# Decay-weighted graph aggregation on one core: decay weights from a scan per row, against decay weights from counts made by matmuls

## The chip, the core and the metric

The kernel runs on one core of a Trainium2 chip. Engines: PE (TensorE, matrix products), DVE (VectorE), ACT (ScalarE), POOL (GpSimd) and SP, which here only issues loads. The time is the device time of one execution in microseconds; the kernel before took 437.13 us (median of three runs, 437.13 to 437.59).

## The reference

```python
h = jnp.maximum(_layernorm(x, axis=-1), 0.0)        # x is (4096, 64)
support = h @ weight                                # weight is (64, 64)
mask = (adj != 0).astype(support.dtype)             # adj is (4096, 4096), fp32
rank = jnp.cumsum(mask, axis=1)
deg = rank[:, -1:]
k = jnp.minimum(deg, float(MAX_NEIGH))              # MAX_NEIGH = 100
pos = rank - (deg - k)
w = mask * jnp.where(pos > 0, DECAY ** (k - pos), 0.0)   # DECAY = 0.5
return x + (w @ support + bias)
```

A neighbour of row i with c neighbours behind it in the same row gets the weight 2^-c, and 0 from the hundredth on. `adj` is 67 MB and is the only large input.

## The kernel before

Rows of `adj` go through in 32 tiles of 128 rows. A tile is one load of 2 MB (`a_sb`, L165, three buffers, issued by SP). Two DVE instructions make the weights of a tile. The mask (L167) writes `f`, 1/2 at a neighbour and 1 elsewhere, in bf16. The scan (L169) runs along each row from its end, `S[j] = max(f[j] * S[j+1], floor)`, in bf16, in one of two buffers. The weight is a difference, S[j+1] - S[j].

PE needs the weights with the column of `adj` on the partitions. For each of 32 column blocks of a tile it multiplies two shifted pieces of S by the identity and by minus the identity and adds them in PSUM (L177, L178): transpose and difference at once. ACT copies eight blocks at a time to SBUF as bf16 (`wT`, L179). PE then multiplies each block with the support of its 128 columns (L148, 192 columns, since the fp32 support is three bf16 parts). The result `po` of a tile is copied by ACT (L153), and POOL adds the three parts and x plus bias (L157, L158, L159) and stores four tiles at a time (L161).

Ahead of this stand the loads of x, weight and bias on ACT's queue (L61 to L66), the layernorm on DVE (L88 to L107), its transpose on PE (L118), the product with the weight (L131) and the split into three parts (L134 to L137). Each engine takes its instructions in the order in which the framework put them; on DVE the layernorm stands among the first masks and scans.

Of the kernel before, what the change touches and what calls it, by code (L numbers as in the profile page):

```python
# [19 lines left out]
def kernel(  # L20
# [50 lines left out]
    ident_b = const.tile([P, P], BF16, name="ident_b")
    nc.gpsimd.tensor_copy(ident_b, ident)
    nident_b = const.tile([P, P], BF16, name="nident_b")
    nc.gpsimd.tensor_scalar_mul(nident_b, ident, -1.0)
    floor_sb = const.tile([P, 1], F32, name="floor_sb")
    nc.gpsimd.memset(floor_sb, 2.0 ** -(MAX_NEIGH - 1))
    S_bufs = []
    for b in range(2):
        S = const.tile([P, N + 1], BF16, name=f"S{b}")
        nc.gpsimd.memset(S[:, N:N + 1], 2.0)  # L80
        S_bufs.append(S)

# [1 line left out]
    def rows(t):  # L84
        return t.unsqueeze(2).to_broadcast([P, C, D])

    mean = setup.tile([P, C], F32, name="mean")
    nc.vector.reduce_sum(mean, x_sb, axis=AX.X)  # L88
    nc.vector.tensor_scalar_mul(mean, mean, 1.0 / D)
    xc = setup.tile([P, C, D], F32, name="xc")  # L90
    nc.vector.tensor_sub(xc, x_sb, rows(mean))  # L91
    sq = setup.tile([P, C, D], F32, name="sq")
    nc.scalar.activation(sq, xc, AF.Square)  # L93
    var = setup.tile([P, C], F32, name="var")
    nc.vector.reduce_sum(var, sq, axis=AX.X)
    nc.vector.tensor_scalar(var, var, 1.0 / D, EPS, op0=ALU.mult, op1=ALU.add)
    # 1 / sqrt(var), with a Newton step for the last bits: y * (1.5 - 0.5 * var * y * y)
    rstd = setup.tile([P, C], F32, name="rstd")
    nc.scalar.activation(rstd, var, AF.Sqrt)
    nc.vector.reciprocal(rstd, rstd)  # L100
    corr = setup.tile([P, C], F32, name="corr")
    nc.vector.tensor_mul(corr, var, rstd)
    nc.vector.tensor_mul(corr, corr, rstd)
    nc.vector.tensor_scalar(corr, corr, -0.5, 1.5, op0=ALU.mult, op1=ALU.add)
    nc.vector.tensor_mul(rstd, rstd, corr)
    hn = setup.tile([P, C, D], F32, name="hn")
    nc.vector.tensor_mul(hn, xc, rows(rstd))  # L107

    xb = const.tile([P, C, D], F32, name="xb")
    nc.gpsimd.tensor_add(xb, x_sb, bias_sb.unsqueeze(1).to_broadcast([P, C, D]))  # L110

# [1 line left out]
    hT = setup.tile([P, C // 2, P], F32, name="hT")  # L113
    for g in range(C // 2 // G):
        pt = ps_t.tile([P, G, P], F32, tag="pt", name=f"pth{g}")
        for k in range(G):
            a = g * G + k
            nc.tensor.transpose(pt[:, k, :], hn[:, 2 * a:2 * a + 2, :].rearrange("p c d -> p (c d)"), ident)  # L118
        nc.scalar.activation(hT[:, g * G:(g + 1) * G, :], pt, AF.Relu)  # L119

    sup = const.tile([P, C, 3, D], BF16, name="sup")
    CS = G * P // D
    for g in range(C // CS):
        pt = ps_t.tile([P, G, P], F32, tag="pt", name=f"pts{g}")
        # the two row halves of hT go to one bank each
        pv = pt.rearrange("p (s h) (q d) -> p s (h q) d", s=2, d=D)
        part = sup[:, g * CS:(g + 1) * CS].rearrange("p (k s) e d -> p s k e d", s=2)
        for k in range(CS // 2):
            a = g * (CS // 2) + k
            for s in range(2):  # L130
                nc.tensor.matmul(pv[:, s, k, :], hT[s * D:(s + 1) * D, a, :], w_sb[s * D:(s + 1) * D, :],  # L131
                                 start=True, stop=True)
        rest = setup.tile([P, 2, CS // 2, D], F32, name="rest", bufs=2)
        nc.scalar.activation(part[:, :, :, 0, :], pv, AF.Copy)  # L134
        nc.vector.tensor_sub(rest, pv, part[:, :, :, 0, :])  # L135
        nc.scalar.activation(part[:, :, :, 1, :], rest, AF.Copy)
        nc.vector.tensor_sub(part[:, :, :, 2, :], rest, part[:, :, :, 1, :])  # L137

# [1 line left out]
    out_t = out.rearrange("(c p) d -> p c d", p=P)  # L140
    osb = None
    pending = None

    def aggregate(po, wT, t, g):
        nonlocal osb
        for k in range(G):
            c = g * G + k
            nc.tensor.matmul(po, wT[:, c, :], sup[:, c].rearrange("p s d -> p (s d)"),  # L148
                             start=(c == 0), stop=(c == C - 1))
        if g < NG - 1:  # L150
            return
        parts = work.tile([P, 3, D], F32, name="parts")
        nc.scalar.activation(parts, po.rearrange("p (s d) -> p s d", d=D), AF.Copy)  # L153
        if t % OG == 0:
            osb = work.tile([P, OG, D], F32, name="osb")
        o = osb[:, t % OG, :]
        nc.gpsimd.tensor_add(parts[:, 1, :], parts[:, 1, :], parts[:, 2, :])  # L157
        nc.gpsimd.tensor_add(parts[:, 0, :], parts[:, 0, :], parts[:, 1, :])  # L158
        nc.gpsimd.tensor_add(o, parts[:, 0, :], xb[:, t, :])  # L159
        if t % OG == OG - 1:  # L160
            nc.gpsimd.dma_start(out_t[:, t - OG + 1:t + 1, :], osb)  # L161
# [50 lines left out]
```

## Time and profile before

| | |
|---|---|
| median of three runs | 437.13 us |
| span of the profiled execution | 435.5 us |
| time around the span (median less span) | 1.6 us |
| DVE busy | 370.5 us, 85% of the span |
| POOL busy | 331.3 us, 76% |
| PE busy | 255.4 us, 59% |
| ACT busy | 148.8 us, 34% |
| mean granted TensorE clock | 0.863 of full speed |
| loads of adj | 67.11 MB, 42.1% of the time of the 16 DMA engines |

Busy time counts an engine as busy from the start of an instruction to its end, whether it computes or is held. Matmuls overlap, so PE's mean duration of one is longer than the distance between two starts; rates are read from starts. In the timeline, "x8" is a run of eight like instructions, the second number is the length of the run, and "[... <-...]" is the idle time ahead and what ended it.

### The profile page before, as it was taken

To read this page: it belongs to the slowest core of one execution; us is meant where nothing else is said; L and a number is where in the kernel's file an instruction comes from. 1 tells how busy PE (TensorE), PEld (TensorE's weight loads), DVE (VectorE), ACT (ScalarE), POOL (GpSimd) and SP (SyncE) were. 2 spreads that over 40 slices of the span, in tenths; PEclk is the share of its full clock that TensorE was granted. 3 is DMA by queue.
4 is the path that set the end of the run, shared out by engine and by line. 5 is a ranking of instruction groups with operands and counts; after the bars stand their busy time and mean duration, and the time that the engine had idled before them with its cause. 6 is when DMAs were issued, how large, how long until landed. Compare 5 with 4: busy or idle time off the path is not lost.

```text
span 435.5 us, 6885 instructions
## 1 busy us (share of the span) xinstructions
PE 255.4 (59%) x3152; PEld 245.7 (56%) x3152; DVE 370.5 (85%) x79; ACT 148.8 (34%) x171; POOL 331.3 (76%) x116
## 2 busy tenths in 40 slices
PE   0000029857749666877748549578387569585394
PEld 0000028857639556766648549567387568585383
DVE  0089974999997997999979998999989979999570
ACT  0011107534415405434225314344064036251253
POOL 1040000699999997999999996999999969999752
PEclk9999999988887968888669788987888869698798
DMA  8914850055555555355553455555554553300000
GB/s 322 350 32 170 337 206 36 2 194 194 193 194 206 193 194 190 111 184 196 181 191 148 182 193 206 194 193 194 194 206 172 191 188 102 135 2 2 12 2 12
DMA packets 6365, 69.70 MB, mean 160 GB/s; under 512 B 961, under 2 KB 1985, under 8 KB 2241
## 3 DMA queue, kind: packets, MB, share of 16 engines
q1 hardware_dynamic: 4608, 67.11, 42.1%
q10 hardware_dynamic: 1344, 1.11, 1.1%
q0 software_dynamic: 384, 1.05, 0.7%
q8 instruction: 24, 0.39, 0.4%
q14 instruction: 5, 0.03, 0.0%
HBM read 68.22 MB, written 1.05 MB: 159 GB/s over the span
## 4 chain that ended last, share of the span: by engine, by line
POOL 69%; PE 8%; DVE 7%; issue 5%; DMA 5%; ACT 4%; POOLq 0%; ACTq 0%
POOL osb L159 26%; POOL parts L157 23%; POOL parts L158 20%; DMA x_sb<-in_x_dram 5%; PE po L148 3%; DVE f L167 3%; ACT wT L179 2%; DVE S L169 2%; PE pt L177 2%; PE pt L178 2%; PE pts L131 1%; PE pth L118 1%; ACT parts L153 1%; POOL out_dram L161 1%; DVE hn L107 1%
## 5 line engine op out<-in xcount | busy, mean ns | idle before, releaser
L169 DVE TENSOR_TENSOR_SCAN S<-f,floor_sb 128x4096 bf16<-128x4096 bf16 x32 | 280.9, 8779 | 19.3 <-PE pt L178 19.3
L177 PE MATMUL pt<-ident_b,S 128*128 128x128 bf16 x1024 | 152.9, 242 | 64.8 <-DVE S L169 64.3
L179 ACT ACTIVATE wT<-pt 128x1024 bf16<-128x1024 f32 x128 | 130.1, 1024 | 156.0 <-PE pt L178 156.0
L157 POOL TENSOR_TENSOR parts<-parts 128x64 f32<-128x64 f32 x32 | 114.6, 3581 | 71.0 <-ACT parts L153 70.9
L178 PE MATMUL pt<-nident_b,S 128*128 128x128 bf16 x1024 | 152.4, 241 | 0.0
L177 PEld LDWEIGHTS <-S 128*128 128x128 bf16 x1024 | 112.8, 111 | 69.8 <-DVE S L169 69.5
L148 PE MATMUL po<-sup,wT 128*128 128x192 bf16 x1024 | 124.9, 274 | 46.4 <-ACT wT L179 46.3
L148 PEld LDWEIGHTS <-wT 128*128 128x128 bf16 x1024 | 97.9, 110 | 49.8 <-ACT wT L179 48.0
L159 POOL TENSOR_TENSOR osb<-parts,xb 128x64 f32<-128x64 f32 x32 | 115.0, 3595 | 2.5
L178 PEld LDWEIGHTS <-S 128*128 128x128 bf16 x1024 | 113.0, 110 | 0.8 <-issue 0.6
L158 POOL TENSOR_TENSOR parts<-parts 128x64 f32<-128x64 f32 x32 | 90.1, 2815 | 2.5
L167 DVE TENSOR_SCALAR f<-a_sb 128x4096 bf16<-128x4096 f32 x32 | 76.8, 2402 | 1.0
L118 PE MATMUL pth<-ident,hn 128*128 128x128 f32 x16 | 3.6, 423 | 63.1 <-DVE hn L107 63.1
L118 PEld LDWEIGHTS pth<-ident,hn 128*128 128x128 f32 x16 | 3.3, 227 | 63.0 <-issue 63.0
L153 ACT ACTIVATE parts<-po 128x192 f32<-128x192 f32 x32 | 10.5, 329 | 62.4 <-POOL osb L159 59.6
L88 DVE TENSOR_REDUCE mean<-x_sb 128x32 f32<-128x2048 f32 x1 | 2.3, 2286 | 22.9 <-DMA x_sb<-in_x_dram 22.9
L110 POOL TENSOR_TENSOR xb<-x_sb,bias_sb 128x2048 f32<-128x2048 f32 x1 | 4.5, 4495 | 22.1 <-DMA bias_sb<-in_L_gnn_bias_dram 22.1
L135 DVE TENSOR_TENSOR rest<-pts,sup 128x1024 f32<-128x1024 f32 x2 | 2.5, 1226 | 7.6 <-ACT sup L134 7.6
L93 ACT ACT_TABLE_LOAD x1 | 1.3, 1283 | 21.0 <-issue 21.0
L93 ACT ACTIVATE sq<-xc 128x2048 f32<-128x2048 f32 x1 | 1.9, 1909 | 18.9 <-DVE xc L91 18.9
L161 POOL DMA_DIRECT2D out_dram<-osb x8 | 6.3, 792 | 2.4 <-POOL osb L159 2.4
L119 ACT ACTIVATE hT<-pth 128x1024 f32<-128x1024 f32 x2 | 2.0, 1024 | 8.3 <-PE pth L118 8.3
(28 smaller groups left out, 26.3 us busy)
## 6 DMA issues: line engine op xcount, KB each, us to landing
a_sb<-in_adj_dram SPq DMA_DIRECT2D x32, 2048.0 KB, 8.0
out_dram<-osb POOLq DMA_DIRECT2D x8, 128.0 KB, 6.1
w_sb<-in_L_gnn_weight_dram ACTq DMA_DIRECT2D x2, 16.0 KB, 12.1
...
```

Of the source, the lines that this page charges most:

```text
L118: nc.tensor.transpose(pt[:, k, :], hn[:, 2 * a:2 * a + 2, :].rearrange("p c d -> p (c d)"), ident)
L148: nc.tensor.matmul(po, wT[:, c, :], sup[:, c].rearrange("p s d -> p (s d)"), start=(c == 0), stop=(c == C - 1))
L153: nc.scalar.activation(parts, po.rearrange("p (s d) -> p s d", d=D), AF.Copy)
L157: nc.gpsimd.tensor_add(parts[:, 1, :], parts[:, 1, :], parts[:, 2, :])
L158: nc.gpsimd.tensor_add(parts[:, 0, :], parts[:, 0, :], parts[:, 1, :])
L159: nc.gpsimd.tensor_add(o, parts[:, 0, :], xb[:, t, :])
L161: nc.gpsimd.dma_start(out_t[:, t - OG + 1:t + 1, :], osb)
L167: nc.vector.tensor_scalar(f, a_sb, 0.0, 0.5, op0=ALU.is_equal, op1=ALU.max)
L169: nc.vector.tensor_tensor_scan(S[:, 0:N][:, ::-1], f[:, ::-1], floor_sb.to_broadcast([P, N]), 2.0, op0=ALU.mult, op1=ALU.max)
L177: nc.tensor.matmul(pt[:, k, :], S[:, j + 1:j + 1 + P], ident_b, start=True, stop=False)
L178: nc.tensor.matmul(pt[:, k, :], S[:, j:j + P], nident_b, start=False, stop=True)
L179: nc.scalar.activation(wT[:, g * G:(g + 1) * G, :], pt, AF.Copy)
```

## The change

The scan goes. Rows of `adj` are taken in eight groups of 512 rows: a tile holds the rows p * 32 + t for the partitions p, and four tiles make a group. The kernel gets the weights by counting:

- `load`: a load of 2 MB into one of four buffers, then one DVE instruction that writes 0 or 1 as fp8, column e * 1024 + q at byte 4q + e, so that four columns share a 32-bit word.
- `turn`: PE transposes the words as fp32 (eight transposes of 128x128 a tile), and DVE copies the words to `mt`. There `plane(g, b)` is the mask of column block b for the 512 rows of a group, one byte in four.
- `totals`: 32 matmuls with 32 stationary columns each (on quarters of the output in turn) give counts of neighbours per block. Two DVE instructions turn them into an fp8 operand `dg`.
- `scan`: for each block two products accumulate in PSUM, a triangular stationary with the mask, and a stationary that carries the later blocks with `dg`. ACT applies relu, multiplies by 128 and writes 16-bit integers, whose bits are the bf16 weight 2^-c.
- `aggregate`: the products with the layernormed, scaled x, not yet multiplied by the weight matrix. Two of its three parts go as one stationary of 128 columns, the third as 64 columns on one half of the output.
- `finish`: the sum is multiplied by the weight matrix, and x plus bias is added by DVE.

The work on the next group (`load`, `turn`, `totals`) lies between the steps of the present one. The two products of L118 and L131 at the start are gone; x is loaded a second time in the order of the output rows. The diff, without the added constants (built by some thirty small instructions on POOL and DVE) and with the layernorm's unchanged steps left out:

```diff
-    apool = ctx.enter_context(tc.tile_pool(name="apool", bufs=3))
-    ps_t = ctx.enter_context(tc.tile_pool(name="ps_t", bufs=3, space=bass.MemoryType.PSUM))
-    ps_o = ctx.enter_context(tc.tile_pool(name="ps_o", bufs=2, space=bass.MemoryType.PSUM))
+    E = 4
+    Q = N // E
+    CB = Q // P
+    TG = 4
+    W = TG * P
+    NP = B // 2
+    LAG = 4
+    apool = ctx.enter_context(tc.tile_pool(name="apool", bufs=4))
+    mpool = ctx.enter_context(tc.tile_pool(name="mpool", bufs=2))
+    wpool = ctx.enter_context(tc.tile_pool(name="wpool", bufs=LAG + 4))
+    ps_t = ctx.enter_context(tc.tile_pool(name="ps_t", bufs=2, space=bass.MemoryType.PSUM))
+    ps_v = ctx.enter_context(tc.tile_pool(name="ps_v", bufs=2, space=bass.MemoryType.PSUM))
+    ps_a = ctx.enter_context(tc.tile_pool(name="ps_a", bufs=1, space=bass.MemoryType.PSUM))
+    ps_m = ctx.enter_context(tc.tile_pool(name="ps_m", bufs=1, space=bass.MemoryType.PSUM))
+    adj_v = adj.rearrange("(p t) n -> p t n", t=RT)
+    xr_sb = const.tile([P, RT, D], F32, name="xr_sb")
+    nc.scalar.dma_start(xr_sb, x.rearrange("(p t) d -> p t d", t=RT))
...
+    nc.gpsimd.tensor_copy(wt[:, 1:, :], later.unsqueeze(2).to_broadcast([P, B, P]), saturate=False)
...
+        nc.vector.tensor_scalar(xc, xc, 0.0, 2.0 ** 27, op0=ALU.max, op1=ALU.mult)
+        nc.scalar.activation(sup[:, :, 0, :], xc, AF.Copy)
+        nc.vector.tensor_sub(xc, xc, sup[:, :, 0, :])
+        nc.scalar.activation(sup[:, :, 1, :], xc, AF.Copy)
+        nc.vector.tensor_sub(sup[:, :, 2, :], xc, sup[:, :, 1, :])
+        nc.gpsimd.tensor_add(xb, xr_sb, bias_sb.unsqueeze(1).to_broadcast([P, RT, D]))
...
+    def load(g, tt):
         a_sb = apool.tile([P, N], F32, name="a_sb")
-        nc.sync.dma_start(a_sb, adj[t * P:(t + 1) * P, :])
-        nc.vector.tensor_scalar(f, a_sb, 0.0, 0.5, op0=ALU.is_equal, op1=ALU.max)
-        nc.vector.tensor_tensor_scan(S[:, 0:N][:, ::-1], f[:, ::-1], floor_sb.to_broadcast([P, N]), 2.0,
-                                     op0=ALU.mult, op1=ALU.max)
+        nc.sync.dma_start(a_sb, adj_v[:, g * TG + tt, :])
+        m8 = mpool.tile([P, Q, E], FP8, name="m8")
+        nc.vector.tensor_scalar(m8.rearrange("p q e -> p e q"), a_sb.rearrange("p (e q) -> p e q", e=E),
+                                0.0, None, op0=ALU.not_equal, saturate=False)
+    def turn(g, tt, h):
...
+        for k in range(CB // 2):
+            c = h * (CB // 2) + k
+            nc.tensor.transpose(pt[:, k, :], m32[:, c * P:(c + 1) * P], ident)
+        nc.vector.tensor_copy(mw[:, h * (CB // 2):(h + 1) * (CB // 2), tt * P:(tt + 1) * P], pt.bitcast(U32))
+    def plane(g, b):
+        return masks[g][:, b % CB, :, b // CB]
+    def totals(g):
+        tot = ps_m.tile([P, W], F32, tag="m", name="tot")
+        for k in range(B // 4):
+            for q in range(4):
+                nc.tensor.matmul(tot[32 * q:32 * q + 32, :], band[:, 31 - k:63 - k], plane(g, 4 * k + q),
+                                 start=(k == 0), stop=(k == B // 4 - 1))
+        nc.vector.tensor_scalar(hi, tot, one31, None, op0=ALU.add, saturate=False)
+        nc.vector.scalar_tensor_tensor(dg, hi, sgn, tot, op0=ALU.mult, op1=ALU.add, saturate=False)
+    def scan(g, k):
+        v = ps_v.tile([P, 2, W], F32, name="v")
+        for s in range(2):
+            b = 2 * k + s
+            nc.tensor.matmul(v[:, s, :], wt[:, 0, :], plane(g, b), start=True, stop=False)
+            nc.tensor.matmul(v[:, s, :], wt[:, 1 + b, :], dgs[g], start=False, stop=True)
+        wk = wpool.tile([P, 2, W], BF16, name="wk")
+        nc.scalar.activation(wk.bitcast(I16), v, AF.Relu, scale=128.0)
+    def aggregate(g, k):
...
+        for s in range(2):
+            nc.tensor.matmul(acc, sup[:, 2 * k + s, 0:2, :].rearrange("p s d -> p (s d)"), wk[:, s, :],
+                             start=(k == 0 and s == 0), stop=False, skip_group_check=True)
+        for s in range(2):
+            nc.tensor.matmul(acc[s * D:(s + 1) * D, :], sup[:, 2 * k + s, 2, :], wk[:, s, :],
+                             start=False, stop=(k == NP - 1), skip_group_check=True)
+    def finish(g):
+        nc.scalar.activation(acc, accs.pop(g), AF.Copy)
+        for tt in range(TG):
+            nc.tensor.matmul(po[:, tt, :], acc[:, tt * P:(tt + 1) * P], w_sb, start=True, stop=True)
+        nc.vector.tensor_add(o, po, xb[:, g * TG:(g + 1) * TG, :])
+        nc.gpsimd.dma_start(out_v[:, g * TG:(g + 1) * TG, :], o)
+    for tt in range(TG):
+        load(0, tt)
+        turn(0, tt, 0)
+        turn(0, tt, 1)
+        if tt == 0:
+            layernorm()
+    totals(0)
+    for g in range(G):
+        for k in range(NP):
+            if g + 1 < G and k % 4 == 0:
+                load(g + 1, k // 4)
+            scan(g, k)
+            if k >= LAG:
+                aggregate(g, k - LAG)
+            if g + 1 < G and k % 2 == 1:
+                turn(g + 1, k // 4, k // 2 % 2)
+        if g + 1 < G:
+            totals(g + 1)
+        for k in range(NP - LAG, NP):
+            aggregate(g, k)
+        finish(g)
```

DVE at the start of the program, before. The rows are instructions in their order, output first; the last two numbers are partitions and elements.

```order
L88 TENSOR_REDUCE mean<-x_sb 128x32
L167 TENSOR_SCALAR f<-a_sb 128x4096
L89 TENSOR_SCALAR mean<-mean 128x32
L169 SCALAR_TENSOR_TENSOR S_91<-f,floor_sb 128x4096
L91 TENSOR_TENSOR xc<-x_sb,mean 128x2048
L167 TENSOR_SCALAR f<-a_sb 128x4096 x2
```

The same place in the change; `m_138` and `m_180` are the fp8 masks of the first two tiles, and the small ones build constants.

```order
L176 TENSOR_SCALAR m_138<-a_sb 128x4x1024
L118 SCALAR_TENSOR_TENSOR blk<-pf 128x1
L120 TENSOR_SCALAR one_120<-pf 128x1
L122 TENSOR_SCALAR lt_122<-pf 128x1
L124 TENSOR_SCALAR lt_124<-pf 128x1
L142 TENSOR_REDUCE mean<-x_sb 128x32
L126 TENSOR_TENSOR sgn<-lt_124,lt_122 128x1
L130 TENSOR_SCALAR later<-later,blk,lt_122 128x32
L127 TENSOR_TENSOR sgn<-sgn,one_120 128x1
L189 COPY mt<-pt 128x4x128
```

One mask now stands ahead of the first instruction that reads x, and the copies of the first tile's words behind it.

PE in the middle of the program, before: the last block of a piece of S, and the first product of the piece before it.

```order
L177 LDWEIGHTS S0_91
L177 MATMUL pt4_3_726<-ident_b_85,S0_91 128x128
L178 LDWEIGHTS S0_91
L178 MATMUL pt4_3_726<-nident_b_87,S0_91 128x128
L148 LDWEIGHTS wT_640
L148 MATMUL po_641<-sup_138,wT_640 128x192
```

The same engine in the change, inside the first group: four transposes of words of the next group, then one pair of blocks (`v_341`), and the aggregation of an earlier pair (`wk_293`).

```order
L188 MATMUL pt_335<-ident_94,m8_310 128x128 x4
L210 LDWEIGHTS wt_105
L210 MATMUL v_341<-mt_140,wt_105 128x512
L211 LDWEIGHTS wt_105
L211 MATMUL v_341<-dg_261,wt_105 128x512
...
L222 LDWEIGHTS sup_134
L222 MATMUL acc_319<-wk_293,sup_134 128x512
...
L225 LDWEIGHTS sup_134
L225 MATMUL acc_319<-wk_293,sup_134 64x512
```

In place of two matmuls of 128 columns and one of 192 for each block of a tile, there are four of 512 columns (two of the scan, one of each kind of the aggregation) for each block of a group, with transposes of the next group between them.

## Rows read from the trace of the kernel before

**Rows 1.** Chain of waits, shares of the span by engine.
```profile
POOL 69%; PE 8%; DVE 7%; issue 5%; DMA 5%; ACT 4%; POOLq 0%; ACTq 0%
```
**Rows 2.** Timeline of DVE and POOL; start and length in us, engine, line.
```profile
132.23 0.32 POOL L158 TENSOR_TENSOR parts<-parts 128x64 f32<-128x64 f32 x1
...
189.62 2.29 DVE L167 TENSOR_SCALAR f<-a_sb 128x4096 bf16<-128x4096 f32 x1
189.66 2.43 POOL L157 TENSOR_TENSOR parts<-parts 128x64 f32<-128x64 f32 x1
...
191.83 8.80 DVE L169 TENSOR_TENSOR_SCAN S<-f,floor_sb 128x4096 bf16<-128x4096 bf16 x1
...
192.17 8.58 POOL L158 TENSOR_TENSOR parts<-parts 128x64 f32<-128x64 f32 x1
...
200.67 2.29 DVE L167 TENSOR_SCALAR f<-a_sb 128x4096 bf16<-128x4096 f32 x1
```
**Rows 3.** Waits: who for whom, us in total, times, longest.
```profile
PE pt L177 <- DVE S L169: 64.3, 23, 4.7
```
**Rows 4.** Timeline of the start.
```profile
1.68 19.41 ACTq L64 DMA_DIRECT2D w_sb<-in_L_gnn_weight_dram  x2
...
22.95 2.29 DVE L88 TENSOR_REDUCE mean<-x_sb 128x32 f32<-128x2048 f32 x1 [22.95 <-DMA x_sb<-in_x_dram]
24.30 4.50 POOL L110 TENSOR_TENSOR xb<-x_sb,bias_sb 128x2048 f32<-128x2048 f32 x1 [22.07 <-DMA bias_sb<-in_L_gnn_bias_dram]
25.16 5.79 DVE L167 TENSOR_SCALAR f<-a_sb 128x4096 bf16<-128x4096 f32 x1
...
60.64 2.29 DVE L107 TENSOR_TENSOR hn<-xc,rstd 128x2048 f32<-128x2048 f32 x1
...
63.08 3.65 PE L118 MATMUL pth<-ident,hn 128*128 128x128 f32 x16 [63.08 <-DVE hn L107]
```
**Rows 5.** DMA queues: packets, MB, share of the 16 engines.
```profile
q1 hardware_dynamic: 4608, 67.11, 42.1%
```
**Rows 6.** Stretch from 8 to 12 us; last three: PEclk, DMA share, GB/s.
```profile
8.00:12.00 4.00, 0.00 (x0) 0.00 (x0) 0.00 (x0) 0.00 (x0) 0.00 (x0) 1.00 0.98 392
```
**Rows 7.** Groups by line: busy us, mean ns of one, idle before.
```profile
L179 ACT ACTIVATE wT<-pt 128x1024 bf16<-128x1024 f32 x128 | 130.1, 1024 | 156.0 <-PE pt L178 156.0
...
L135 DVE TENSOR_TENSOR rest<-pts,sup 128x1024 f32<-128x1024 f32 x2 | 2.5, 1226 | 7.6 <-ACT sup L134 7.6
...
L72 POOL CAST ident_b<-ident 128x128 bf16<-128x128 f32 x1 | 0.3, 288 | 0.1
```
**Rows 8.** Timeline of PE in two pieces.
```profile
190.94 1.49 PE L148 MATMUL po<-sup,wT 128*128 128x192 bf16 x8
192.22 0.31 PE L177 MATMUL pt<-ident_b,S 128*128 128x128 bf16 x1
...
195.01 0.22 PE L178 MATMUL pt<-nident_b,S 128*128 128x128 bf16 x1
...
195.29 0.82 PE L148 MATMUL po<-sup,wT 128*128 128x192 bf16 x8
195.95 0.22 PE L177 MATMUL pt<-ident_b,S 128*128 128x128 bf16 x1
```
**Rows 9.** Timeline of PE, matmuls active from 70.40 (first) and 70.58 (others).
```profile
70.20 0.50 PE L131 MATMUL pts<-w_sb,hT 64*128 64x64 f32 x6
...
70.31 0.39 PE L131 MATMUL pts<-w_sb,hT 64*128 64x64 f32 x4
70.63 0.23 PE L177 MATMUL pt<-ident_b,S 128*128 128x128 bf16 x1
```
**Rows 10.** Timeline of the end.
```profile
431.65 0.77 POOL L161 DMA_DIRECT2D out_dram<-osb  x1 [0.29 <-POOL osb L159]
```
**Rows 11.** Two stretches: PE, PEld, DVE, ACT, POOL busy, PEclk, DMA share, GB/s.
```profile
211.00:222.00 11.00, 6.88 (x64) 6.53 (x64) 10.96 (x3) 1.02 (x1) 10.84 (x3) 0.66 0.54 192
300.00:311.00 11.00, 6.94 (x106) 6.54 (x103) 10.97 (x3) 3.07 (x3) 10.84 (x3) 1.00 0.52 186
```

More of the change, by code (lines that the diff above doesn't have):

```diff
@@ L10 @@
 BF16 = mybir.dt.bfloat16
+FP8 = mybir.dt.float8e4
+I16 = mybir.dt.int16
+I32 = mybir.dt.int32
+U32 = mybir.dt.uint32
 AF = mybir.ActivationFunctionType
@@ L16 @@
 EPS = 1e-5
+DIAG = 104.0
 @with_exitstack
@@ L66 @@
     nc.scalar.dma_start(bias_sb, bias.rearrange("(o d) -> o d", o=1).to_broadcast([P, D]))
+    xr_sb = const.tile([P, RT, D], F32, name="xr_sb")
+    nc.scalar.dma_start(xr_sb, x.rearrange("(p t) d -> p t d", t=RT))
     ident = const.tile([P, P], F32, name="ident")
     make_identity(nc, ident)
[L71 to L81, printed above, removed]
-    def rows(t):
[L85 to L137, printed above, removed]
@@ L140 @@
[L140 to L161, printed above, removed]
@@ L183 @@
-    aggregate(*pending)
+    tri = setup.tile([P, P], F32, name="tri")
+    nc.gpsimd.memset(tri, -1.0)
+    nc.gpsimd.affine_select(out=tri, in_=tri, compare_op=ALU.is_gt, fill=0.0, base=0,
+                            pattern=[[-1, P]], channel_multiplier=1)
+    nc.gpsimd.affine_select(out=tri, in_=tri, compare_op=ALU.not_equal, fill=DIAG, base=0,
+                            pattern=[[-1, P]], channel_multiplier=1)
+    wt = const.tile([P, 1 + B, P], FP8, name="wt")
+    nc.gpsimd.tensor_copy(wt[:, 0, :], tri, saturate=False)
@@ new lines @@
+    band = const.tile([P, 80], FP8, name="band")
+    nc.gpsimd.memset(band, 0.0)
+    nc.gpsimd.memset(band[:, 31:32], 1.0)
+    nc.gpsimd.memset(band[:, 39:40], 1.0)
+    pi = setup.tile([P, 4], I32, name="pi")
+    nc.gpsimd.iota(pi[:, 0:1], pattern=[[0, 1]], base=0, channel_multiplier=1)
+    nc.vector.tensor_scalar(pi[:, 1:2], pi[:, 0:1], 31, None, op0=ALU.bitwise_and)
+    nc.vector.tensor_scalar(pi[:, 2:3], pi[:, 0:1], 7, None, op0=ALU.bitwise_and)
+    nc.vector.tensor_scalar(pi[:, 3:4], pi[:, 0:1], 5, None, op0=ALU.logical_shift_right)
@@ new lines @@
+    pf = setup.tile([P, 4], F32, name="pf")
+    nc.vector.tensor_copy(pf, pi)
+    blk = setup.tile([P, 1], F32, name="blk")
+    nc.vector.scalar_tensor_tensor(blk, pf[:, 2:3], 4.0, pf[:, 3:4], op0=ALU.mult, op1=ALU.add)
+    one31 = const.tile([P, 1], F32, name="one31")
+    nc.vector.tensor_scalar(one31, pf[:, 1:2], 31.0, None, op0=ALU.is_equal)
+    lt16 = setup.tile([P, 1], F32, name="lt16")
+    nc.vector.tensor_scalar(lt16, pf[:, 1:2], 16.0, None, op0=ALU.is_lt)
+    lt8 = setup.tile([P, 1], F32, name="lt8")
@@ new lines @@
+    nc.vector.tensor_scalar(lt8, pf[:, 1:2], 8.0, None, op0=ALU.is_lt)
+    sgn = const.tile([P, 1], F32, name="sgn")
+    nc.vector.tensor_sub(sgn, lt8, lt16)
+    nc.vector.tensor_add(sgn, sgn, one31)
+    later = setup.tile([P, B], F32, name="later")
+    nc.gpsimd.iota(later, pattern=[[1, B]], base=0, channel_multiplier=0, allow_small_or_imprecise_dtypes=True)
+    nc.vector.tensor_scalar(later, later, blk, lt16, op0=ALU.is_lt, op1=ALU.mult)
+    nc.vector.tensor_scalar(later, later, one31, -1.0, op0=ALU.add, op1=ALU.mult)
@@ new lines, with layernorm @@
+    nc.gpsimd.tensor_copy(wt[:, 1:, :], later.unsqueeze(2).to_broadcast([P, B, P]), saturate=False)
+    sup = const.tile([P, B, 3, D], BF16, name="sup")
+    xb = const.tile([P, RT, D], F32, name="xb")
+    def rows(t):
+        return t.unsqueeze(2).to_broadcast([P, B, D])
+    def layernorm():
+        mean = setup.tile([P, B], F32, name="mean")
+        nc.vector.reduce_sum(mean, x_sb, axis=AX.X)
+        nc.vector.tensor_scalar_mul(mean, mean, 1.0 / D)
+        xc = setup.tile([P, B, D], F32, name="xc")
+        nc.vector.tensor_sub(xc, x_sb, rows(mean))
+        sq = setup.tile([P, B, D], F32, name="sq")
+        nc.scalar.activation(sq, xc, AF.Square)
+        var = setup.tile([P, B], F32, name="var")
+        nc.vector.reduce_sum(var, sq, axis=AX.X)
+        nc.vector.tensor_scalar(var, var, 1.0 / D, EPS, op0=ALU.mult, op1=ALU.add)
+        rstd = setup.tile([P, B], F32, name="rstd")
+        nc.scalar.activation(rstd, var, AF.Sqrt)
+        nc.vector.reciprocal(rstd, rstd)
+        corr = setup.tile([P, B], F32, name="corr")
+        nc.vector.tensor_mul(corr, var, rstd)
+        nc.vector.tensor_mul(corr, corr, rstd)
+        nc.vector.tensor_scalar(corr, corr, -0.5, 1.5, op0=ALU.mult, op1=ALU.add)
+        nc.vector.tensor_mul(rstd, rstd, corr)
+        nc.vector.tensor_mul(xc, xc, rows(rstd))
+        nc.vector.tensor_scalar(xc, xc, 0.0, 2.0 ** 27, op0=ALU.max, op1=ALU.mult)
[4 more added lines that the diff above has]
+        nc.gpsimd.tensor_add(xb, xr_sb, bias_sb.unsqueeze(1).to_broadcast([P, RT, D]))
```

45 lines of the change are left out of this document (24 added, 21 removed).

## The prediction, made before the changed kernel was run

> **What bounds the kernel now.** I read the chain of waits first. It gives POOL 69% of the span [rows 1], but the timeline of one tile takes that back: POOL's adds of 64 elements last 8.58 us beside a scan, 2.43 us beside a mask, and 0.32 us where neither runs [rows 2]. They end when DVE's instruction ends, so POOL is held and DVE sets the pace: mask 2.29 us, scan 8.80 us, and the next tile 11.05 us after the last (189.62 to 200.67 [rows 2]). Thirty-two such tiles make 354 of the 435.5 us. TensorE waits for the scans (23 waits, 64.3 us, the longest 4.7 [rows 3]). The rest is the start: DVE sits until x lands at 22.95 us and TensorE begins at 63.08 us [rows 4]. The loads alone, 67.11 MB [rows 5] at the 392 GB/s of an early stretch [rows 6], would take 171 us.
>
> The span is 435.5 us and the median of the runs 437.13, so 1.6 us lie around the span.
>
> **What goes.** The 32 scans (282 us of DVE at 8.80), POOL's adds, and 3,072 matmuls of 128 and 192 columns.
>
> **What DVE, ACT and the loads get, per group of 512 rows.** DVE: four masks at 2.29 us [rows 2], eight copies of 512 words out of PSUM, two count instructions, one add. For PSUM sources the nearest row is 1.23 us for 1,024 elements [rows 7], so I take 0.69 for 512. Sum 9.2 + 5.5 + 1.4 + 0.4 = 16.5 us. The mask now writes single bytes four apart, which no row shows. If it lost half its speed the sum would be 26 us; if it gained as much, 12. ACT: sixteen instructions of 1,024 at 1.02 us [rows 7] and a copy, 17 us. Loads: 8.4 MB, 21 us. All stay below what TensorE needs (next part), so these edits cost nothing in the loop. Were TensorE twice as fast as I think, loads and DVE would be next, near 21 us a group.
>
> **TensorE, per group.** Six starts, five of 128-column matmuls and then the first of 192, go from 195.01 to 195.29: 55 ns each. Eight of 192 columns take 0.66 us (195.29 to 195.95), 82.5 ns each [rows 8]. That is 0.42 ns for each further column, so 217 ns for 512.
> - Scan (L210, L211): 64 of 512 columns, 13.9 us. Aggregation with full stationaries (L222): 32, 6.9 us.
> - Aggregation with 64 stationary columns (L225): 32, issued in pairs on the two output halves. The only row on parts of the array is L131, pairs on row halves: their starts, two by two, are 0.11 us apart (70.20, 70.31 [rows 9]), the time of one four-pass matmul of 64 columns (4 x 64 x 0.42 = 108 ns). Two cost one there. I take that for column halves: 16 x 0.217 = 3.5 us. One after the other it is 6.9.
> - Counts (L198): 32 of 512 columns with 32 stationary columns, on the four quarters of the output in turn. Side by side 8 x 0.217 = 1.7 us, one after the other 6.9. I take 1.9.
> - Turning the words (L188): 32 fp32 transposes, as L118: 16 in 3.65 us [rows 4], 228 ns each, 7.3 us.
> - Projection (L233): four fp32 matmuls of 64 columns, 0.45 us.
> - Changing between whole array and halves, twice for each of 16 pairs. The last pair of L131 starts at 70.42, one step after 70.31, and would release the array at 70.53. The first full matmul starts at 70.63 [rows 9], so one change costs 0.10 us: 3.2 us a group. Bounds: nothing, or a matmul's fill (0.23 [rows 9] less 0.055, 0.17) and one more step like the 0.10, 0.27.
>
> The Trainium skill (TensorEngine Tiling (Array Packing), Key Properties) says that a change of tiling mode drains TensorE; it gives no price. The 0.10 us of [rows 9] agree. By the rule the changes cannot be hidden; without it the 26 us that they make over eight groups would go and the sum would be 334.
>
> A group's own work is 13.9 + 6.9 + 3.5 + 0.45 + 3.2 = 27.9 us, and the preparation of the next 7.3 + 1.9 = 9.2, together 37.1. Eight of the first and seven of the second, less 1.8 us for eight transposes that the start already does: 223 + 64 - 2 = 285 us. Waits inside are small as ordered. The counts of the next group are followed by 13 matmuls (some 2.4 us) before its first scan, beside the 1.4 us of the two count instructions. ACT, at a group's start with four scans and no aggregation, needs 4 x 1.02 + 0.6 us against 5.7 us of TensorE. Were such cover gone, it would be 1 to 2 us a group.
>
> **The start.** Three tiles were asked for at once, and x landed at 22.95 [rows 4], about when 6.3 MB of tiles and 1 MB of x at 392 GB/s are through (19 us and some latency). Now there are four buffers. The first mask stands ahead of x's reduction on DVE, frees its buffer early and so starts a fifth load, while everything behind the reduction waits for x. Two more tiles are 4.2 MB, 10.7 us: x lands between 22.9 and 33.6. I take 31, since x came last before. The weights, bias and the second copy of x stand behind it on ACT's queue (19.41 us of issue [rows 4]). POOL's add and its cast of 4,096 elements follow, some 10.5 us (4.50 for the add [rows 4], 6 for the cast by the 0.29 of one of 128 [rows 7]), and end before the first scan. But a mask beside POOL's add took 5.79 us in place of 2.29 [rows 4], so I add 4 us (0 to 10).
>
> DVE's chain from x to the last copy of group 0: mean, centring, variance and product, 9.2 (four of 2,048 elements, the first and the last with 2.29 each in [rows 4]); three masks 6.9; eight copies 5.5; the relu 1.2; a dozen small ones 2.2; gaps 1; POOL 4. That is 30 us, to 61. Then the counts (2), with one mask and one subtraction (2.3 each), a copy and the two count instructions (0.7 each) queued on DVE: the scan starts at 68. Bounds 56 (x as early as before, no contention) and 78.
>
> **The end.** Copy 0.5, projection 0.5, add 0.5, issue 0.8, and the 3.1 us from the last output's issue to the end now (431.65 + 0.77 to 435.5 [rows 10]): 5.5 us.
>
> Sum: 68 + 285 + 5.5 = 358.5 in the span, 360 with what lies around it. With every low bound 56 + 285 - 26 + 7 = 322. With every high one, tiles still side by side, 78 + 285 + 43 + 7 = 413.
>
> **Rivals.**
> 1. Column tiles don't run side by side. For it: the only pairs seen are on row halves, each with inputs of its own rows. L225 adds 3.5 us a group and the counts 5, eight times: +68, 428 us. Against it: [rows 9] show that the array takes two instructions at once.
> 2. Masks read with a step of four bytes halve TensorE's rate. No row has such an operand. L210 then costs 6.9 us more a group, the counts 1.7: +69, 429 us.
> 3. Loads become the bound. Before, a tile was one block of 2 MB; now its 128 rows lie 32 rows, 512 KB, apart. Were that half the 392 GB/s of [rows 6], x would land near 55 us and the loop start at 92; 42 us of loads a group against 37.1 of TensorE; the last tile at 340, and behind it a mask, its turn, the counts, one group of 28 us and the end, 45 us: about 385. Loads decide only below 8.4 / 37.1, 226 GB/s. The Trainium skill (DMA: Bandwidth & Descriptors, Latency and other measured facts) gives 207 GB/s for tiles of 128 rows of 16 KB with a pitch of 512 KB, between tensors in HBM; by it the loads take 324 us and the time would be about 370 to 385. No run here shows that pitch.
> 4. Slower: TensorE at its lower level, 1.2 GHz. There eight of 192 columns take 1.28 us (190.94 to 192.22 [rows 8]) for 0.66. The granted clock was 0.66 in a stretch with 6.9 us of TensorE's work in 11, and 1.00 in another with as much [rows 11]. The waits for scans [rows 3], which surround the falls, are gone from the loop. If the loop ran at 0.66 its 285 us would be 432, in all 507. It turns to slower than 437 below a mean of 285 / 362 = 0.79.
>
> **Chances.** Forecast 0.60, rival 1 0.13, rival 2 0.07, rival 3 0.12, rival 4 0.08. About 0.2% (0.9 us) either way is what can be told from no change. Rivals 1 and 2 end some 9 us below the present time and may miss: I leave 0.02 of them within 0.2% and 0.02 above. Faster 0.88, same 0.02, slower 0.10. The range 322 to 430 holds the forecast's own 322 to 413, rival 3 and most of 1 and 2.
>
> **What would show it.** In the new trace: x landing near 31 and the first L211 near 68; starts of L210 and L211 217 ns apart (434 for L210: rival 2); a pair of L225 in about 0.22 us (0.43: rival 1); L188 at 228 ns; the granted clock at 1.00 through the loop; DVE, ACT and DMA each below 60% busy there, TensorE over 90%; a group every 37 us. Tiles landing at 200 GB/s, or TensorE idle for a mask, would make the price of loads or DVE wrong.

## The result, and the profile after

The changed kernel took 339.74 us (median of four runs, 338.82 to 340.04), the kernel before in the same comparison 437.36. The ratio is 0.774 (95% interval 0.770 to 0.779). 360 was forecast, in a range of 322 to 430. The profiled execution took 338.82 us, with a span of 337.1 and a mean granted TensorE clock of 0.998.

The chain of waits and the busy times of the page come first. The chain's shares by engine answer to [rows 1]:

```profile
PE 287.7 (85%) x1600; PEld 123.9 (37%) x1600; DVE 158.5 (47%) x146; ACT 143.4 (43%) x143; POOL 19.5 (6%) x25
...
PE 73%; DVE 10%; issue 9%; DMA 7%; ACT 0%; POOLq 0%; POOL 0%
```

TensorE has taken the place of DVE and POOL. The stretches show it more sharply than the average does (us; busy time and count of PE, PEld, DVE, ACT, POOL; PEclk; DMA share; GB/s; they answer to [rows 6, 11]):

```profile
8.00:12.00 4.00, 0.83 (x4) 0.86 (x5) 2.65 (x5) 0.00 (x0) 0.00 (x0) 1.00 1.03 418
56.50:91.50 35.00, 34.20 (x186) 13.52 (x186) 21.32 (x16) 17.17 (x18) 0.00 (x0) 1.00 0.74 295
125.00:160.00 35.00, 35.00 (x200) 15.05 (x200) 17.45 (x15) 16.87 (x17) 0.55 (x1) 1.00 0.62 243
```

From 125 to 160 us TensorE is never idle, and its granted clock is 1.00 (2.4 GHz); DVE and ACT are half idle. At 8 to 12 us tiles whose rows lie 512 KB apart land at 418 GB/s, no slower than the 392 of [rows 6].

The projections of the chain (start, length, line) mark the end of each group:

```profile
91.69 0.84 PE po L233 x8
126.86 0.84 PE po L233 x8
```

A group takes 35.17 us (37.1 was forecast). One stretch of TensorE's timeline gives the prices inside it, by the distance from start to start, as in [rows 8]:

```profile
100.77 0.59 PE L222 MATMUL acc<-wk,sup 128*128 128x512 bf16 x2
101.29 0.41 PE L225 MATMUL acc<-wk,sup 128*64 128x512 bf16 x2
101.63 0.40 PE L210 MATMUL v<-mt,wt 128*128 128x512 fp8e4 x1
101.87 0.38 PE L211 MATMUL v<-dg,wt 128*128 128x512 fp8e4 x1
102.08 0.39 PE L210 MATMUL v<-mt,wt 128*128 128x512 fp8e4 x1
...
103.05 0.41 PE L225 MATMUL acc<-wk,sup 128*64 128x512 bf16 x2
103.39 0.65 PE L188 MATMUL pt<-ident,m 128*128 128x128 f32 x4
103.88 0.39 PE L210 MATMUL v<-mt,wt 128*128 128x512 fp8e4 x1
```

From L210, whose operand has a step of four bytes, to the next start are 0.225 to 0.24 us, from L211 0.215. Two L222 and the change behind them take 0.52; the pair of L225 and its change back 0.34, less than two matmuls of 0.215 one after the other. Four transposes take 0.49 us, 0.12 each; at L118 one took 0.228 [rows 4].

At the end of a group the counts part one pair of L225, so that its two products run alone:

```profile
120.81 0.40 PE L225 MATMUL acc<-wk,sup 128*64 128x512 bf16 x1
121.14 1.77 PE L198 MATMUL tot<-mt,band 128*32 128x512 fp8e4 x28
122.85 0.40 PE L225 MATMUL acc<-wk,sup 128*64 128x512 bf16 x1
```

By the distances between all starts of one group (126.70 to 161.87) the scan takes 14.2 us, the aggregation with its changes 14.2, the transposes 3.9, the counts 2.05 and the projection 0.84, together 35.2.

The start, as in [rows 4] (start, length; idle time ahead and what ended it in brackets):

```profile
8.59 2.43 DVE L176 TENSOR_SCALAR m<-a_sb 128x4096 fp8e4<-128x4096 f32 x1 [6.16 <-DMA a_sb<-in_adj_dram]
11.17 1.94 PE L188 MATMUL pt<-ident,m 128*128 128x128 f32 x8 [11.17 <-DVE m L176]
...
22.82 2.29 DVE L142 TENSOR_REDUCE mean<-x_sb 128x32 f32<-128x2048 f32 x1 [11.58 <-DMA x_sb<-in_x_dram]
...
28.48 7.28 POOL L167 TENSOR_TENSOR xb<-xr_sb,bias_sb 128x2048 f32<-128x2048 f32 x1 [25.85 <-DMA xr_sb<-in_x_dram]
...
32.50 5.55 DVE L176 TENSOR_SCALAR m<-a_sb 128x4096 fp8e4<-128x4096 f32 x1
...
50.18 2.67 PE L198 MATMUL tot<-mt,band 128*32 128x512 fp8e4 x28 [0.15 <-DVE mt L189]
...
56.83 0.38 PE L211 MATMUL v<-dg,wt 128*128 128x512 fp8e4 x1 [2.92 <-DVE dg L203]
```

x lands at 22.82 us, as before (22.95), and the first L211 starts at 56.83. SP's queue tells why x is not later (who for whom, us, times, longest):

```profile
SPq L174 <- DVE m L176: 207.2, 26, 10.8
...
SPq L174 <- DMA x_sb<-in_x_dram: 20.7, 1, 20.7
```

The fourth load, for which a buffer is free, waits 20.7 us for x, though it does not need x. In the trace's records it signals on the same semaphore as x, which was issued eight loads before it in the two queues of ACT and SP. So three tiles are ahead of x, not five. The end, as in [rows 10]:

```profile
330.53 0.41 PE L225 MATMUL acc<-wk,sup 128*64 128x512 bf16 x2
330.98 0.60 ACT L230 ACTIVATE acc_sb<-acc 128x512 f32<-128x512 f32 x1 [3.19 <-PE acc L225]
331.62 1.10 PE L233 MATMUL po<-w_sb,acc_sb 128*128 128x64 f32 x8 [0.69 <-ACT acc_sb L230]
...
333.49 0.54 POOL L236 DMA_DIRECT2D out_dram<-o  x1 [28.62 <-DVE o L235]
```

### The profile page after: what moved, and what is told of

The parts are those of the page before. It is cut to its first block, busy times and chain, and to the rows that moved or that the text cites. A ratio compares the mean times of both kernels' runs of the same rounds, so it can differ in the third digit from the quotient of the medians.

```text
span 337.1 us, 3778 instructions
## 1 busy us (share of the span) xinstructions
PE 287.7 (85%) x1600; PEld 123.9 (37%) x1600; DVE 158.5 (47%) x146; ACT 143.4 (43%) x143; POOL 19.5 (6%) x25
## 4 chain that ended last, share of the span: by engine, by line
PE 73%; DVE 10%; issue 9%; DMA 7%; ACT 0%; POOLq 0%; POOL 0%
PE v L210 17%; PE acc L222 15%; PE v L211 14%; PE acc L225 12%; PE pt L188 9%; DMA x_sb<-in_x_dram 7%; PE tot L198 4%; DVE m L176 4%; PE po L233 2%; DVE mt L189 2%; DVE xc L160 1%; DVE mean L142 1%; DVE xc L145 1%; DVE xc L164 1%; DVE var L149 1%
## 5 line engine op out<-in xcount | busy, mean ns | idle before, releaser
L213 ACT ACTIVATE wk<-v 128x1024 int16<-128x1024 f32 x128 | 130.1, 1024 | 93.7 <-PE v L211 93.6
L210 PE MATMUL v<-mt,wt 128*128 128x512 fp8e4 x256 | 99.9, 391 | 0.5 <-ACT wk L213 0.5
L211 PE MATMUL v<-dg,wt 128*128 128x512 fp8e4 x256 | 96.4, 377 | 2.9 <-DVE dg L203 2.9
L189 DVE COPY mt<-pt 128x512 uint32<-128x512 uint32 x64 | 44.1, 690 | 101.9 <-PE pt L188 101.8
L176 DVE TENSOR_SCALAR m<-a_sb 128x4096 fp8e4<-128x4096 f32 x32 | 85.8, 2685 | 6.2 <-DMA a_sb<-in_adj_dram 6.2
L188 PE MATMUL pt<-ident,m 128*128 128x128 f32 x256 | 43.5, 301 | 39.3 <-DVE m L176 34.3
L222 PE MATMUL acc<-wk,sup 128*128 128x512 bf16 x256 | 76.6, 379 | 0.0
L225 PE MATMUL acc<-wk,sup 128*64 128x512 bf16 x256 | 54.8, 403 | 0.0
L188 PEld LDWEIGHTS pt<-ident,m 128*128 128x128 f32 x256 | 30.6, 151 | 52.9 <-issue 46.1
L210 PEld LDWEIGHTS <-wt 128*128 128x128 fp8e4 x256 | 24.8, 97 | 35.2 <-issue 17.2
L225 PEld LDWEIGHTS <-sup 128*64 128x64 bf16 x256 | 14.7, 106 | 57.4 <-issue 57.4
L222 PEld LDWEIGHTS <-sup 128*128 128x128 bf16 x256 | 22.0, 96 | 31.2 <-issue 7.3
L211 PEld LDWEIGHTS <-wt 128*128 128x128 fp8e4 x256 | 24.8, 97 | 18.6 <-issue 1.5
```

The lines of the kernel that those rows point to most:

```text
L176: nc.vector.tensor_scalar(m8.rearrange("p q e -> p e q"), a_sb.rearrange("p (e q) -> p e q", e=E), 0.0, None, op0=ALU.not_equal, saturate= ...
L188: nc.tensor.transpose(pt[:, k, :], m32[:, c * P:(c + 1) * P], ident)
L189: nc.vector.tensor_copy(mw[:, h * (CB // 2):(h + 1) * (CB // 2), tt * P:(tt + 1) * P], pt.bitcast(U32))
L210: nc.tensor.matmul(v[:, s, :], wt[:, 0, :], plane(g, b), start=True, stop=False)
L211: nc.tensor.matmul(v[:, s, :], wt[:, 1 + b, :], dgs[g], start=False, stop=True)
L213: nc.scalar.activation(wk.bitcast(I16), v, AF.Relu, scale=128.0)
```

## The experiments

All are edits of the changed kernel. The last column is the distance between the projections of two groups in the middle of the loop. Each was timed in five rounds beside the kernel before, whose medians in these comparisons reach from 437 to 440 us, so differences of a microsecond or two between rows of the table mean little.

| edit | us | ratio to before, 95% interval | group, us |
|---|---|---|---|
| changed kernel | 339.74 | 0.774 (0.770 to 0.779) | 35.17 |
| 1 one small load more | 335.06 | 0.764 (0.761 to 0.768) | 35.17 |
| 2 one load fewer | 354.64 | 0.809 (0.806 to 0.812) | 35.17 |
| 3 x ahead of the tiles | 332.12 | 0.758 (0.755 to 0.761) | 35.17 |
| 4 matmuls added in the start | 339.68 | 0.775 (0.772 to 0.778) | 35.17 |
| 5 third part over the whole array | 335.02 | 0.764 (0.760 to 0.767) | 34.58 |
| 6 halves gathered in eights | 314.96 | 0.719 (0.715 to 0.723) | 32.10 |
| 7 no third part | 285.62 | 0.651 (0.647 to 0.654) | 28.48 |
| 8 masks written twice | 349.3 | 0.796 (0.792 to 0.800) | 36.01 |
| 9 third part on one half | 365.01 | 0.831 (0.827 to 0.835) | 38.37 |
| 10 edits 3 and 6 | 308.66 | 0.702 (0.698 to 0.705) | 32.10 |
| 11 edit 10 and a later add | 304.18 | 0.692 (0.689 to 0.696) | 32.09 |

### 1 to 3: what sets the arrival of x

```diff
 # 1
+    nc.scalar.dma_start(spare, weight)
 # 2
-    nc.scalar.dma_start(bias_sb, ...)
+    nc.gpsimd.dma_start(bias_sb, ...)
 # 3
-    nc.scalar.dma_start(x_sb, ...)
+    nc.sync.dma_start(x_sb, ...)
```

> One more small load makes the third tile's load, not the fourth's, wait for x, so two tiles are ahead of x in place of three. Theory A (x takes turns with the tiles that are in flight, and a tile is 2.1 MB at some 0.40 MB/us): x lands 5 us earlier, near 17.6 us, the third tile 5 us later than now but still before DVE wants it at 32; the first L211 near 52 and the time about 335 us. Theory B (x's 256-byte pieces set its landing whatever is beside it): x stays near 22.8, the time at 339 to 341.

> The bias is loaded from POOL's queue, and now the fifth tile's load, not the fourth's, waits for x: four tiles are ahead of x. Theory A, which the forecast used: x lands 5 us later, near 28, and the scan of the first group and the end move by as much, about 345 us. Theory B: x at 22.8, time 339 to 341.

> x goes out on SP's queue ahead of all tiles. Theory A: with nothing beside it x lands at 5 to 8 us and the tiles come 3 to 6 us later than now, the fourth near 29; DVE does its layernorm while it waits for tiles, the first L211 comes near 40 in place of 57, and the time is about 322 us. Theory B: x takes its 22 us alone, the tiles follow, and the time is 20 us longer, 360. A slower first tile alone would cost at most 5 us.

The first instruction that reads x, in the timelines of the three:

```profile
17.91 2.29 DVE L144 TENSOR_REDUCE mean<-x_sb 128x32 f32<-128x2048 f32 x1 [6.72 <-DMA x_sb<-in_x_dram]
```
```profile
29.48 2.29 DVE L142 TENSOR_REDUCE mean<-x_sb 128x32 f32<-128x2048 f32 x1 [16.28 <-DMA x_sb<-in_x_dram]
```
```profile
8.20 2.29 DVE L142 TENSOR_REDUCE mean<-x_sb 128x32 f32<-128x2048 f32 x1 [5.78 <-DMA x_sb<-in_x_dram]
```

With two, three and four tiles ahead x lands at 17.9, 22.8 and 29.5 us, with none at 8.2 (there on SP's queue): some 5 to 7 us for a tile of 2 MB. Which tile waits for x goes by its place in the sequence of loads, since one small load more or fewer moves it by one; in the changed kernel and in edits 1 and 2 the tile that waits is the eighth load behind x on the queues of ACT and SP. Edit 1 gave its expected 335. Edit 2 missed by 10 us: x came 6.7 later, the first L211 16.2 later (73.04). DVE was busy almost without a pause from x to the last count instruction, and the starts of its instructions divide the other 9.5 us. An instruction of one element lasted until POOL's add was done (4.3 us more than in the changed kernel), one more mask stood ahead of the counts and another took longer (2.9 together), the last subtraction L166 stood ahead of them instead of behind (2.2), and so did one more copy (0.6); 0.4 came back elsewhere.

```profile
33.20 4.42 DVE L126 TENSOR_TENSOR sgn<-lt,lt 128x1 f32<-128x1 f32 x1
```

Edit 3 missed by 10 too, 332 for 322: x came 14.6 us earlier, the first L211 only 6.9 (49.93). Its timeline shows what held DVE:

```profile
12.74 4.98 POOL L167 TENSOR_TENSOR xb<-xr_sb,bias_sb 128x2048 f32<-128x2048 f32 x1 [10.72 <-DMA xr_sb<-in_x_dram]
...
13.27 4.47 DVE L127 TENSOR_TENSOR sgn<-sgn,one 128x1 f32<-128x1 f32 x1
...
17.91 2.44 DVE L176 TENSOR_SCALAR m<-a_sb 128x4096 fp8e4<-128x4096 f32 x1
```

A DVE instruction of one element lasts until POOL's add is done, and the first mask stands behind it. That is 4.3 of the 7.7 us by which the chain from x to the first L211 is longer; 2.2 are L166, here too ahead of the counts. From 17.9 us DVE is busy almost without a pause until the counts. So the start is DVE's chain, behind the later of x and POOL's add. Edit 11 tests this.

### 4: why the transposes cost half

```diff
+        for r in range([0, 24, 24, 16][tt]):
+            nc.tensor.matmul(v[:, r % 2, :], wz, z512, start=True, stop=True)
```

> 64 matmuls of 512 columns on constants are added between the transposes of the first group; their output is not used. Theory: TensorE ran at its lower level until 52 us, so the eight transposes that took 1.94 us at 38 and 45 us take about 1.06 as later on, and the 28 count matmuls at 50 take 1.8 in place of 2.67; DVE's chain hides part, so the time is 1 to 2 us shorter, 338. Rival: transposes are slow at the start for another reason (POOL and DVE busy with SBUF, or each being alone): 1.94 stays, the time stays or grows by 1 us.

Two of the runs of eight transposes (L194 in this kernel), from TensorE's timeline:

```profile
29.37 1.94 PE L194 MATMUL pt<-ident,m 128*128 128x128 f32 x8 [10.78 <-DVE m L182]
38.41 1.07 PE L194 MATMUL pt<-ident,m 128*128 128x128 f32 x8 [0.44 <-DVE m L182]
```

The granted clock in four stretches of this run, each within such a run: the first after TensorE had been idle for 10.8 us, the second right behind added matmuls (31.11 to 37.97 us), the third after an idle time of 2.8 us, the fourth behind the counts. The columns are as in the first stretches above; PEclk is the third from the end.

```profile
29.37:31.10 1.73, 1.73 (x8) 1.68 (x9) 1.73 (x1) 0.00 (x0) 1.73 (x1) 0.50 0.99 426
38.41:39.30 0.89, 0.89 (x8) 0.89 (x9) 0.89 (x1) 0.00 (x0) 0.89 (x1) 1.00 1.03 442
45.32:47.20 1.88, 1.88 (x8) 1.55 (x9) 1.81 (x3) 0.00 (x0) 0.00 (x0) 0.50 0.86 288
53.00:54.00 1.00, 0.94 (x8) 0.93 (x9) 1.00 (x1) 0.00 (x0) 0.00 (x0) 1.00 0.57 147
```

At a granted clock of 0.50 (1.2 GHz) eight take 1.94 us by the timeline, at 1.00 (2.4 GHz) 1.07. POOL was busy in the first two stretches and idle in the last two, DVE busy in all four, so the rival in the expectation falls. The 16 transposes of [rows 4], from which I took 228 ns, start 0.213 us apart in the trace, as do the early ones of the changed kernel; at the full clock it is 0.109. So they ran at the lower level. The time of the whole did not change, where 338 had been expected: DVE sets the start, and the last count instruction `dg` began at 56.25 us for 56.04.

### 5 to 7 and 9: what the third part costs

```diff
 # 5
-            nc.tensor.matmul(acc[s * D:(s + 1) * D, :], sup[:, 2 * k + s, 2, :], ...)
+            nc.tensor.matmul(acc, sup[:, 2 * k + s, 2:4, :], ...)   # fourth part: zeros
 # 6
-    wpool = ...(tc.tile_pool(name="wpool", bufs=LAG + 4))
+    wpool = ...(tc.tile_pool(name="wpool", bufs=LAG + 8))
+        if k % 4 < 3:
+            return
+        for kk in range(k - 3, k + 1):   # the products of L225 for four pairs together
 # 7: L225 left out
 # 9
-            nc.tensor.matmul(acc[s * D:(s + 1) * D, :], ...)
+            nc.tensor.matmul(acc[0:D, :], ...)
```

> The third part of the support goes as a full stationary of 128 columns, 64 of them zero, so no matmul of the aggregation uses halves of the array and none of the changes is left there. Theory (two halves side by side, and 0.09 to 0.12 us for each change): 16 pairs cost 0.21 us less for changes and 0.217 more for the second matmul, so a group is as long as before within 0.3 us and the time 338 to 343. Rival (halves run one after the other, no price for changes): nothing changes either, so this run alone does not tell; with e6 it does. Rival (changes free, halves side by side): 3.5 us a group more, 367.

> The matmuls on halves of the array are gathered: those of four pairs in a row, so 8 changes a group in place of 32. Theory (0.09 to 0.12 us a change): 24 x 0.105 = 2.5 us less a group, 20 us in all, about 320. Rival (changes free and halves one after the other): no change, 340.

> The third part of the support is left out of the aggregation, so the output lacks it. If TensorE's starts set the end everywhere in the loop, 128 times the 0.34 us from the start of a pair to the next matmul and the 0.09 us of the change ahead of it go: 55 us less, about 285. If another engine is close behind (ACT 17 us, DVE 17, loads 21 a group against 28 left), nothing of this is lost; a smaller gain would name that engine.

> Both products of the third part (L225) go to the same 64 output columns, so that they cannot run beside each other; the third part's sum is thereby partly in the wrong half, all else as in the changed kernel. Theory A (the pair on two halves runs side by side): each of the 128 pairs becomes 0.217 us longer, +27.8 us: 367.5 us, a group every 38.6 us. Theory B (they run one after the other already, and the trace's starts mislead): 340 us.

TensorE's timeline with both products on one half, then with eight of them gathered:

```profile
152.00 0.62 PE L225 MATMUL acc<-wk,sup 128*64 128x512 bf16 x2
152.56 0.40 PE L210 MATMUL v<-mt,wt 128*128 128x512 fp8e4 x1
```
```profile
153.11 1.05 PE L229 MATMUL acc<-wk,sup 128*64 128x512 bf16 x8
154.09 0.40 PE L210 MATMUL v<-mt,wt 128*128 128x512 fp8e4 x1
```

On one half the pair takes 0.56 us in place of 0.34, and a group is 3.20 us longer (15 x 0.213, since one of the sixteen pairs is parted anyway; 16 x 0.217 had been expected): the pairs did run side by side. Eight gathered ones take 0.98 us, four steps of 0.215 and one change. In the changed kernel a group has 36 changes, 32 between whole array and halves and four to or from the quarters of the counts. Gathering takes 24 of them away and puts the parted pair together, for 3.07 us: (3.07 less 0.215) / 24 = 0.119 us each. Edit 5 gives the same price by another way. It takes 32 changes away, adds 15 products of 0.215, and the group is 0.59 us shorter: (3.23 + 0.59) / 32 = 0.119. Both did better than expected (338 to 343, about 320), since 0.105 had been taken and the parted pair overlooked. A pair on halves with its two changes, 0.215 + 0.24, is a little dearer than two products over the whole array. Edit 6 also has four more buffers for `wk`, but in the changed kernel TensorE waits for `wk` only 0.5 us in all. Edit 7 shows that what TensorE starts sets the time: 54 us less, for 55 expected.

### 8: whether DVE is off the path

```diff
+        if g > 0:   # the mask (L176) once more
+            nc.vector.tensor_scalar(m8..., a_sb..., 0.0, None, op0=ALU.not_equal, saturate=False)
```

> DVE makes each mask twice from the second group on. 28 more instructions of 2.4 to 2.6 us, 70 us of DVE. Theory (off the path in the loop): the only cost is one or two of them that stand ahead of the counts of the first group, 0 to 3 us, so 339 to 343. Rival (DVE holds the transposes' buffers or the loads and so the loop): some us a group, 350 or more.

It took 6 to 10 us longer than expected, 349.3: 0.84 us more a group, and the first projection 6.3 us later (97.83 for 91.53 in the timelines). A boundary of two groups, first in the changed kernel, then with the second mask (L179):

```profile
120.65 2.63 DVE L176 TENSOR_SCALAR m<-a_sb 128x4096 fp8e4<-128x4096 f32 x1
...
123.94 0.75 DVE L203 SCALAR_TENSOR_TENSOR dg<-hi,sgn,tot 128x512 fp8e4<-128x512 fp8e4 x1
...
126.04 0.38 PE L211 MATMUL v<-dg,wt 128*128 128x512 fp8e4 x1
```
```profile
129.67 2.61 DVE L179 TENSOR_SCALAR m<-a_sb 128x4096 fp8e4<-128x4096 f32 x1
...
132.13 0.78 DVE L204 TENSOR_SCALAR hi<-tot,one 128x512 fp8e4<-128x512 f32 x1
...
132.94 0.75 DVE L206 SCALAR_TENSOR_TENSOR dg<-hi,sgn,tot 128x512 fp8e4<-128x512 fp8e4 x1
...
133.84 1.08 PE L236 MATMUL po<-w_sb,acc_sb 128*128 128x64 f32 x8
134.75 0.38 PE L214 MATMUL v<-dg,wt 128*128 128x512 fp8e4 x1
```

In the changed kernel `dg` is ready at 124.69, 1.4 us ahead of the matmul that reads it. With one mask more ahead of the count instructions it is ready at 133.69; the projection, which needs the buffer of the counts, and the scan start right behind it. So DVE is half idle and still has only some 1.4 us of slack at each boundary. In the start `dg` came 3.95 us later (59.99 for 56.04), behind a second mask. The other 2.3 of the 6.3 us are TensorE's lower level. TensorE had been idle for 5.2 us ahead of 58.05, its granted clock was 0.50, and the first products of the scan, from 60.78 to 65.85 us, start 0.42 us apart in place of 0.22 (same columns as in the stretches above):

```profile
60.78:66.00 5.22, 5.00 (x12) 1.82 (x13) 5.22 (x4) 2.81 (x3) 0.00 (x0) 0.50 0.69 295
```

### 10 and 11: the gains put together

```diff
 # 10: edits 3 and 6; 11: also
-    nc.scalar.dma_start(xr_sb, ...)
-        nc.gpsimd.tensor_add(xb, xr_sb, ...)
+                if g == 0 and k == 4:   # behind load(1, 1)
+                    nc.sync.dma_start(xr_sb, ...)
+                    nc.gpsimd.tensor_add(xb, xr_sb, ...)
```

> Both single edits at once: third parts in eights (315.0 us alone) and x ahead of the tiles (7.6 us off alone). Theory A (start and loop add up, TensorE sets the loop): 307.3 us, first L211 at 50, a group every 32.1 us. Theory B (once TensorE takes less a group, the loads or DVE hold the loop, so that a part of the earlier start is lost in waits for tiles): 310 to 315.

> As the one before, and the second copy of x is loaded behind the sixth tile, so that POOL's add of x and bias runs after the start. Theory A (in the start DVE is held by POOL's add: there a DVE instruction of one element took 4.47 us): the first mask starts at 13 to 14 in place of 17.9, the first L211 4 us earlier, at 46, time 303. Theory B (the first tile lands only then, so the hold costs nothing): first mask at 17, time 306 to 307.

Start and loop add up: 308.66, for 307.3 expected. Without POOL's add in the start DVE's instruction of one element and the first mask read:

```profile
13.41 0.15 DVE L126 TENSOR_TENSOR sgn<-sgn,one 128x1 f32<-128x1 f32 x1
...
13.62 2.61 DVE L174 TENSOR_SCALAR m<-a_sb 128x4096 fp8e4<-128x4096 f32 x1
```

4.47 us have become 0.15, and the count instruction `dg` comes 4.3 us earlier (44.82 for 49.10). At 304.18 us this version is ahead of both kernels.

## Why the prediction was right, and where it was off

| term | forecast | measured |
|---|---|---|
| x lands | 31 | 22.82 |
| DVE from x until group 0 is turned | 30 | 27.3 (50.18, where the last counts begin, less 0.1 and 22.82) |
| from there to the first L211 | 7 | 6.7 |
| loop, to the last L225 | 285 | 274 (56.83 to 330.9) |
| end | 5.5 | 6.2 |
| around the span | 1.6 | 1.7 (338.82 less 337.1) |

**What held.** TensorE took the bound, and its price by starts was right: 0.215 to 0.24 us for 512 columns in all four kinds of product, for 0.217; scan 14.2 us a group (forecast 13.9), aggregation and its changes 14.2 (13.6), counts 2.05 (1.9). POOL, which was 76% busy before, is busy for 0.55 us in 35 of the loop. DVE's 17.4 and ACT's 16.9 us a group lay beside TensorE's work as forecast (16.5 and 17). Of the cover for the two count instructions 1.4 us were left, where 1.0 had been forecast (2.4 less 1.4); edit 8 used it up, at 0.84 us a group (1 to 2 had been named).

**The step that failed.** "Now there are four buffers. The first mask ... frees its buffer early and so starts a fifth load": neither the fourth nor the fifth load went ahead of x, because the fourth waits for x itself. I counted buffers, and not what else an issue waits for. That made x 8.2 us too late. The price of a tile ahead was near: 5.4 us in the forecast, and edit 2, with four tiles ahead, has x at 29.48, 6.7 later.

**The size that was off.** "32 fp32 transposes, as L118: 16 in 3.65 us": at the full clock they take 3.9 us a group, not 7.3. Edit 4 shows the two levels. The granted clock alone would not have warned me. The first stretch above reads 1.00 while the eight transposes of that time (11.17 us) take 1.94 us, as long as edit 4's at 0.50; the profile has no record of the clock before its first change. Against this stand the aggregation with its changes (0.6 us a group above the forecast), the projections (0.84 for 0.45), the scan (0.3 above) and the counts (0.15 above). In sum a group is 1.9 us below the forecast, the loop 11.

**The change of mode.** 0.12 us by edits 5 and 6, for 0.10, inside the bounds of 0 to 0.27. The forecast counted 32 changes a group and left out the four of the counts, and that the counts part a pair: 36 changes make 4.3 us a group, 12% of it, where 3.2 stood. The starts in the timeline agree with the edits. A pair pays 0.09 ahead of its products (0.52 less two of 0.215) and 0.12 behind (0.34 less 0.215), and the first product after it is late by another 0.01 (L210) to 0.06 us (L188): about 0.245 for the two changes. The Trainium skill (TensorEngine Tiling (Array Packing), Key Properties) says that a change of mode drains TensorE; edits 5 and 6 agree that each change costs time, 0.12 us.

**The rivals.** 1 (column tiles one after the other): refuted by the 0.34 us of a pair and by edit 9. 2 (step of four bytes): refuted, 0.225 to 0.24 us from L210 to the next start. 3 (loads at half rate): refuted by 418 GB/s; from 125 to 160 us TensorE had no gap in which to wait for a tile. The Trainium skill (DMA: Bandwidth & Descriptors, Latency and other measured facts) has 207 GB/s at this pitch for copies within HBM, and 214 for a padded pitch, which it calls full; so it does not call this pitch slow, as the rival took it. For loads into SBUF the measurement decides. 4 (the lower clock): refuted, 1.00 in both stretches of the loop shown.

**A term that did not follow from its row.** "6 for the cast by the 0.29 of one of 128": 32 times 0.29 would be 9.3, and the prediction shows no working for the 6. The cast took 5.79 us, off the path.

So 360 was 20 us too high: 8.2 of x, 3 of DVE's chain, 11 of the loop, less 0.7 of the end and 0.9 by which the median lies above the profiled execution.
